# A new written-out order of the words of all engines and of the transfers in a cross-attention kernel

## The chip, the cores and the metric

One Trainium2 chip, one core of it. The metric is the device time of one execution in microseconds (us), the median of the runs shown. The core has five instruction queues that run side by side and wait for one another by semaphores: TensorE (PE, with its weight loads shown apart as PEld), VectorE (DVE), ScalarE (ACT), GpSimd (POOL) and SyncE (SP), which here only issues DMA transfers. Each queue works strictly in its own program order.

## The reference

All arithmetic is float32. `x` is (2, 2048, 640), the context (2, 154, 1024); 77 of its tokens are text, 77 an image prompt. There are 20 heads of 32.

```python
q = _split_heads(hidden_states @ Wq.T, H)
k = _split_heads(text @ Wk.T, H)
v = _split_heads(text @ Wv.T, H)
out_text = _merge_heads(_attend(q, k, v, sm_scale))
k_ip = _split_heads(ip @ Wk_ip.T, H)
v_ip = _split_heads(ip @ Wv_ip.T, H)
out_ip = _merge_heads(_attend(q, k_ip, v_ip, sm_scale))
out = out_text + IP_SCALE * out_ip
out = out @ Wo.T + bo
return out + residual
```

`_attend` is softmax(q kT / sqrt(32)) v. The two softmaxes are taken over the 77 text and the 77 image keys apart.

## The kernel before, in words

Tokens lie in the free dimension, channels in the partitions. The 640 channels are 5 chunks of 128 (4 heads each). A *quarter* q = 0..9 is one batch element and one chunk; a *unit* u = 2q + sub is one half (1024 tokens, two blocks h of 512) of it. The scores of a unit come in three *groups* s = 0, 1, 2 of 3, 3 and 2 tiles of 128 tokens, 4 heads by 154 keys each.

The whole program after a short head (lines 612 to 671) is one string of 1317 *words*, `SCHEDULE` (line 673), split at blanks and handed one by one to `emit` (line 769). A word issues a few instructions on one engine; the order of the words of one engine in the string is the program order of that engine's queue, and the order across engines tells which value of a reused buffer a word reads. `@` and digits after a word name the PSUM banks (0 to 7) that it writes. Nothing else sets the order. The words that matter here:

- TensorE, on full 128x128 weights: `q.u.h` queries of a block (`queries`, L211), `k.c.t` and `v.c.t` keys and values (L146), `g m.p.i` the products of a Strassen-like scheme for later queries (L281, L291), `m m.b.i` those for the output projection of batch element 0 (L579, L589), `o`, `p`, `z` the fifth output chunk (L560), `F` the closing products for batch element 1 (L1006). I call these wide words.
- TensorE, on 32x128 weights: `R s.u` the scores of a group, into four banks (L323). On 32x32 weights: `A.q` probabilities times values (L421).
- ScalarE: `K s.u` copies the scores to SBUF (L335), `E s.u.g` exponentials (L358, L390), `cq`, `ck`, `cv`, `CA`, and some `cg` empty a bank (L232, L826, L828, L444, L300).
- VectorE: `M` maxima (L370, or L373 straight from the bank), `D` sums of the exponentials (L395), `I` their reciprocals (L400), `T` the 32x32 transposes of the probabilities (L412), `cm`, `co`, `Y`, and some `cg` take a bank (L604, L610, L570, L944, L947, L302).
- GpSimd: `S` subtracts the maxima where that is a step of its own (L384), `N` multiplies with the reciprocals (L405).
- *Sums*, plain additions of two SBUF operands: `U` of query weights (L262), `h` of tokens (L275), `W` of output weights (L490), `G` (L520), `V` and `X` (L985, L991) for the closing products. Those that end in `.d` (and with `V`, `X` those with `.d`) are issued on VectorE, all others on GpSimd.
- SyncE, all transfers: `LK`, `LQ`, `LO`, `LW` weights, `LX`, `LH`, `LA`, `SF` tokens in, `SS` results out, `VS` the spreading of the values to the four row groups (8 small DMAs each). The queue issues in order, and a transfer whose place is still in use holds back all behind it.

For one group of scores the chain is R, K, M, (S), E, D, I, N, T, and once all six groups of a quarter have their T, `A`. TensorE keeps busy with wide words between them.

The change and the steps of the prediction touch `SCHEDULE` alone; these functions, as they stand, carry the words that the prediction names: `queries`, `project_kv`, `scores`, `attend`, `pair_product`, `product`, `take_product`, `store_last`, `sum_pair_tokens`, `sum_w`, `subtract`, `normalise`, `maxima`, `load_block`, `load_wq`. The engine of a sum is settled in `emit`:

```python
adder = nc.vector if args and args[-1] == "d" else nc.gpsimd
```

Of the kernel before, what the change touches and what calls it, by code (L numbers as in the profile page):

```python
# [20 lines left out]
def kernel(  # L21
# [643 lines left out]
    for t in range(2):  # L665
# [8 lines left out]
        "q.0.1@2 R0.0@6457 cq.0.1 R1.0@0132 K0.0 K1.0 q.1.0@6 LK.4 M0.0 LK.5 M1.0 S0.0 LQ.3 R2.0@0132 v.0.0@7 K2.0 "  # L674
        "E0.0.0 E0.0.1 E0.0.2 E0.0.3 M2.0 S1.0 q.1.1@2 cv.0.0 D0.0 E1.0.0 S2.0 I0.0 cq.1.1 E1.0.1 v.0.1@7 N0.0 "
        "cq.1.0 E2.0.0 E2.0.1 E2.0.2 E1.0.2 E1.0.3 D1.0 cv.0.1 E2.0.3 R0.1@1326 LK.7 D2.0 LK.6 K0.1 R1.1@4507 I1.0 "
        "I2.0 SQ.0 N2.0 VS.0.0 K1.1 q.3.0@1 M0.1 M1.1 S0.1 R2.1@4507 K2.1 LQ.4 E0.1.0 M2.1 S1.1 VS.0.1 T0.0 cq.3.0 "
        "q.2.1@6 E2.1.0 E0.1.1 k.1.0@1 E1.1.0 N1.0 T2.0 E2.1.1 E0.1.2 E1.1.1 k.1.1@7 ck.1.0 E0.1.3 cq.2.1 E2.1.2 "
        "ck.1.1 E1.1.2 E1.1.3 D1.1 I1.1 v.1.0@6 T1.0 N1.1 E2.1.3 D0.1 cv.1.0 R2.2@5017 LK.10 SF.0.4 R0.2@3246 K2.2 "
        "LK.8 q.3.1@5 LK.9 D2.1 K0.2 I0.1 T1.1 N0.1 I2.1 M0.2 R1.2@3246 q.4.0@7 N2.1 K1.2 T0.1 S0.2 T2.1 M2.2 "  # L680
        "A.0@3246 E0.2.0 M1.2 S2.2 cq.4.0 E0.2.1 E0.2.2 cq.3.1 E0.2.3 D0.2 E2.2.0 S1.2 I0.2 CA.0 R0.3@0175 N0.2 "
        "K0.3 E2.2.1 v.1.1@3 k.2.1@0 E1.2.0 cv.1.1 E2.2.2 LK.13 ck.2.1 E1.2.1 E2.2.3 E1.2.2 D2.2 I2.2 M0.3 "
        "R2.3@6175 SQ.1 SF.0.3 R1.3@2430 S0.3 K2.3 E1.2.3 D1.2 VS.1.1 q.4.1@6 M1.3 E0.3.0 N2.2 M2.3 E1.3.0 k.2.0@5 "
        "T0.2 S2.3 SF.0.1 E1.3.1 v.2.0@7 VS.1.0 T2.2 E2.3.0 E0.3.1 I1.2 ck.2.0 E2.3.1 E0.3.2 E0.3.3 q.5.0@1 D0.3 "
        "N1.2 cv.2.0 E2.3.2 E1.3.2 cq.4.1 E2.3.3 D2.3 E1.3.3 LK.12 I2.3 I0.3 SF.0.2 T1.2 N2.3 LK.11 SF.0.0 cq.5.0 "
# [12 lines left out]
        "N2.7 cq.10.0 LX.10.1 T1.7 LK.18 K0.8 R1.8@7204 S2.8 K1.8 q.9.1@5 M0.8 T2.7 S0.8 LQ.7 M1.8 E0.8.0 S1.8 "
        "cq.9.1 E0.8.1 v.4.1@4 A.3@6720 E2.8.0 E0.8.2 E1.8.0 E2.8.1 E1.8.1 E0.8.3 E1.8.2 E2.8.2 E2.8.3 E1.8.3 D0.8 "
        "I0.8 D2.8 N0.8 cv.4.1 I2.8 CA.3 R0.9@3154 VS.5.0 D1.8 I1.8 G5.0 K0.9 v.4.0@6 T0.8 R2.9@7203 N2.8 cv.4.0 "  # L700
        "q.11.1@5 SQ.4 M2.9 VS.4.0 N1.8 E2.9.0 M0.9 E2.9.1 E2.9.2 T2.8 S0.9 E2.9.3 R1.9@4672 q.10.1@0 M1.9 LX.12.0 "
        "E1.9.0 I2.9 E0.9.0 E0.9.1 E0.9.2 T1.8 N2.9 E1.9.1 q.11.0@3 LX.12.1 VS.4.1 E1.9.2 E0.9.3 D0.9 E1.9.3 I0.9 "
        "T2.9 N0.9 cq.11.1 D1.9 cq.10.1 R0.10@4672 cq.11.0 K0.10 R1.10@1503 I1.9 T0.9 K1.10 g2.0.0@4 g1.0.0@7 "
        "M0.10 U0.0 N1.9 LO R2.10@6215 cg1.0.0 g2.0.1@0 K2.10 h5.0.0 T1.9 E0.10.0 g1.0.1@1 h7.0.0 g5.0.0@5 E0.10.1 "
        "cg2.0.0 U4.0 M2.10 A.4@3624 U1.0 cg1.0.1 E0.10.2 h6.0.0.d h5.0.1.d M1.10 E0.10.3 h7.0.1 U3.0 cg5.0.0 "
        "E2.10.0 h6.0.1.d S1.10 cg2.0.1 E2.10.1 U2.0.d g3.0.0 VS.6.0 CA.4 g5.0.1@0 g6.0.1 h4.0.1 cg5.0.1 D0.10 "
        "E2.10.2 g6.0.0 h4.0.0 R0.11@3624 cg6.0.0 cg6.0.1 I0.10 cg3.0.0 E2.10.3 g7.0.0 M0.11 N0.10 E1.10.0 g7.0.1 "
        "o.0@5 D2.10 E0.11.0 W0 E0.11.1 cg7.0.0 cg7.0.1 T0.10 E0.11.2 E0.11.3 g4.0.0 co.0 SS.0.4 D0.11 cg4.0.0 "
        "E1.10.1 R1.11@3625 LX.13.0 g3.0.1 K1.11 I0.11 g4.0.1 cg3.0.1 I2.10 M1.11 N2.10 cg4.0.1 R2.11@6250 LX.13.1 "
        "R1.12@4731 K2.11 E1.10.2 m2.0@6 S1.11 K1.12 E1.10.3 M2.11 E2.11.0 cm2.0 R0.12@4731 N0.11 T2.10 K0.12 "  # L710
        "R2.12@2506 g1.0.2@4 M1.12 K2.12 m1.0@3 E2.11.1 h5.0.2.d m5.0@6 G6.0 cm1.0 E1.11.0 D1.10 SS.0.0 h7.0.2 "
        "E2.11.2 E1.11.1 E1.11.2 g5.0.2@0 h6.0.2 M2.12 SF.1.0 g1.0.3@5 cg1.0.2 E2.11.3 h5.0.3.d g6.0.2 I1.10 cm5.0 "
        "h7.0.3 cg5.0.2 E1.11.3 g2.0.2@2 D1.11 cg6.0.2 W1 g7.0.2 g2.0.3@1 cg2.0.2 I1.11 h4.0.2 E1.12.0 E1.12.1 "
        "T0.11 m3.0 LQ.9 N1.10 VS.5.1 E2.12.0 cg7.0.2 cg1.0.3 E2.12.1 cg2.0.3 m2.1@2 M0.12 E1.12.2 h6.0.3 T1.10 "
        "N1.11 g4.0.2 E2.12.2 SF.1.4 m6.0 E2.12.3 cm2.1 I2.11 cm3.0 g6.0.3 N2.11 T1.11 g5.0.3@2 cg6.0.3 E0.12.0 "
        "g3.0.2 h4.0.3 T2.11 cg4.0.2 cg5.0.3 E0.12.1 g7.0.3 G7.0 LX.16.0 A.5@7164 cg7.0.3 D2.12 E0.12.2 U0.1.d "
        "E1.12.3 cm6.0 G4.0.d cg3.0.2 I2.12 E0.12.3 N2.12 m7.0 CA.5 D0.12 R0.13@0716 I0.12 cm7.0 N0.12 g3.0.3 "
        "M0.13 E0.13.0 m4.0 LQ.8 E0.13.1 SS.0.1 cg3.0.3 T0.12 h5.1.0 E0.13.2 g4.0.3 E0.13.3 cm4.0 R1.13@0271 U1.1 "
        "cg4.0.3 I1.12 D0.13 SF.1.1 U4.1 K1.13 R2.13@4635 VS.6.1 U3.1 g1.1.0@0 N1.12 g2.1.0@2 cg1.1.0 M1.13 K2.13 "
        "R2.14@7146 g5.1.0@3 K2.14 I0.13 M2.13 h6.1.0 R1.14@5714 cg5.1.0 T2.12 LX.16.1 h7.1.0 E2.13.0 SS.0.3 o.1@6 "  # L720
        "VS.7.0 M2.14 S1.13 E2.13.1 T1.12 K1.14 E1.13.0 G5.1 cg2.1.0 m1.1@4 co.1 U2.1 M1.14 E2.13.2 E1.13.1 N0.13 "
# [12 lines left out]
        "M0.16 cg2.1.2 SS.1.1 g5.1.3@7 T1.16 S0.16 cg6.1.3 R0.17@0514 cg5.1.3 SF.2.1 SS.1.3 g3.1.3 K0.17 D2.16 "
# [320 lines left out]
```

## Time and profile before

| what | value |
| --- | --- |
| median of 3 runs (lowest, highest) | 490.3 us (489.92, 490.32) |
| span of the profiled execution, first to last instruction | 488.8 us |
| median less span | 1.5 us |
| VectorE busy | 427.2 us, 87% |
| GpSimd busy | 374.0 us, 76% |
| ScalarE busy | 342.1 us, 70% |
| TensorE weight loads, beside the matmuls | 312.0 us, 64% |
| DMA moved | 62.86 MB, mean 129 GB/s |
| transfers issued by SyncE | 291 |

The time of the profiled execution is its span and what lies around it; only the median of the runs is known for that, and it is 1.5 us more than the span. Rows of the chain of waits read: start in us, duration in us, what ran (engine, tile, line, matmul records). Each float32 matmul leaves two records. Rows of the groups read: line, engine, operation, out<-in shapes, count, then busy us and mean ns of one, then idle time of the engine before them and what ended it.

### The profile page before, as it was taken

The numbers are of one execution on the slowest core, as the hardware profiler recorded it, in microseconds if no ns is written. First come the engines' busy times: TensorE is split into PE (matmuls) and PEld (weight loads), VectorE is DVE, ScalarE is ACT, GpSimd is POOL, SyncE is SP. The second block draws the span as 40 slices with busy tenths as digits, with TensorE's granted clock in tenths as the row PEclk, the third lists the DMA queues.
The fourth block names the chain that finished last, engine by engine and source line by source line (L and its number), as shares of the span: only waits on it lengthen the run. The fifth ranks groups of instructions, "written<-read, shape, count | busy, mean of one in ns | idle before, by whom it ended". The sixth has DMA issues, their size and how long they took to land.

```text
span 488.8 us, 11001 instructions
## 1 busy us (share of the span) xinstructions
PE 482.8 (99%) x4244; PEld 312.0 (64%) x4244; DVE 427.2 (87%) x450; ACT 342.1 (70%) x1191; POOL 374.0 (76%) x180
## 2 busy tenths in 40 slices
PE   9999999999999999999999999999999999999996
PEld 5556746657757466566887767787677676444443
DVE  0067998998998989999899899999999999899886
ACT  1267948998699868999898899897979995100000
POOL 0068798887858899888797798899899999369910
PEclk9999999999999999999999999999999999999999
DMA  8994332443061761741623256115130169420026
GB/s 281 351 266 108 83 104 76 132 109 94 18 198 29 235 187 27 232 142 32 214 77 115 78 173 207 56 38 160 48 110 27 45 199 332 130 86 1 21 87 235
DMA packets 63828, 62.86 MB, mean 129 GB/s; under 512 B 5408, under 2 KB 47008, under 8 KB 63776
## 3 DMA queue, kind: packets, MB, share of 16 engines
q1 hardware_dynamic: 62768, 60.99, 40.4%
q10 hardware_dynamic: 1008, 1.18, 0.7%
q8 instruction: 33, 0.54, 0.5%
q14 instruction: 19, 0.16, 0.1%
HBM read 48.38 MB, written 10.49 MB: 120 GB/s over the span
## 4 chain that ended last, share of the span: by engine, by line
PE 91%; ACT 4%; DMA 3%; DVE 1%; ACTq 0%; issue 0%; DVEq 0%
PE bank L211 17%; PE bank L1006 12%; PE bank L281 11%; PE bank L323 10%; PE bank L579 10%; PE bank L421 10%; PE bank L146 8%; PE bank L560 7%; PE bank L589 3%; PE bank L291 3%; ACT pb L358 3%; DMA aT<-in_L_xattn_Wk_ip_dram 2%; DMA x<-in_x_dram 1%; DVE mx L370 1%; ACT pb L335 1%; ACT qT L232 0%
## 5 line engine op out<-in xcount | busy, mean ns | idle before, releaser
L405 POOL TENSOR_TENSOR pb<-pb,rden 128x1848 f32<-128x1848 f32 (+1 forms) x60 | 176.2, 2946 | 33.9 <-DVE rden L400 31.2
L384 POOL TENSOR_TENSOR pb<-pb,mx 128x1848 f32<-128x1848 f32 (+1 forms) x32 | 98.9, 3098 | 37.5 <-DVE mx L370 37.3
L370 DVE TENSOR_REDUCE mx<-pb 128x24 f32<-128x1848 f32 (+1 forms) x51 | 92.8, 1830 | 34.6 <-ACT pb L335 34.5
L412 DVE STREAM_TRANSPOSE pb<-pb 128x1920 f32<-128x1920 f32 (+1 forms) x60 | 114.8, 1926 | 2.1 <-POOL pb L405 1.9
L358 ACT ACTIVATE pb<-pb,mx 128x77 f32<-128x77 f32 x368 | 110.8, 374 | 1.3 <-DVE mx L370 1.2
L335 ACT COPY pb<-bank 128x462 f32<-128x462 f32 (+1 forms) x204 | 86.3, 536 | 17.9 <-PE bank L323 17.7
L395 DVE TENSOR_REDUCE den<-pb 128x24 f32<-128x1848 f32 (+1 forms) x47 | 88.7, 1893 | 8.1 <-ACT pb L390 4.7
L390 ACT ACTIVATE pb<-pb 128x1848 f32<-128x1848 f32 (+1 forms) x32 | 52.5, 1645 | 16.5 <-POOL pb L384 16.4
L421 PE MATMUL bank<-pb,v 32*32 32x512 f32 x1600 | 55.2, 597 | 0.1
L358 ACT ACTIVATE pb<-bank,mx 128x77 f32<-128x77 f32 x200 | 51.4, 373 | 3.5 <-DVE mx L373 3.4
L211 PE MATMUL bank<-x,wq 128*128 128x512 f32 x120 | 53.7, 598 | 0.0
L211 PE MATMUL bank<-x,aT 128*128 128x512 f32 x116 | 52.4, 599 | 0.1
L146 PEld LDWEIGHTS bank<-wo_ct,aT 128*128 128x128 f32 x320 | 43.1, 188 | 5.6 <-issue 3.3
L146 PE MATMUL bank<-wo_ct,aT 128*128 128x154 f32 x320 | 45.6, 296 | 0.8 <-DMA aT<-in_L_xattn_Wk_ip_dram 0.5
L421 PEld LDWEIGHTS bank<-pb,v 32*32 32x32 f32 x1600 | 29.2, 103 | 21.5 <-issue 10.6
L281 PE MATMUL bank<-x,wq 128*128 128x256 f32 x160 | 40.9, 386 | 0.0
L211 PEld LDWEIGHTS bank<-x,wq 128*128 128x128 f32 x120 | 22.1, 190 | 25.5 <-issue 24.7
L211 PEld LDWEIGHTS bank<-x,aT 128*128 128x128 f32 x116 | 21.2, 189 | 24.1 <-issue 23.8
L560 PE MATMUL bank<-aT,wo_ct 128*128 128x512 f32 x80 | 36.4, 596 | 0.0
L358 ACT ACTIVATION_READ_ACCUMULATOR pb<-pb,mx 128x1 f32 x168 | 36.1, 215 | 0.0
L323 PEld LDWEIGHTS bank<-kT,qT 32*128 32x128 f32 x768 | 27.4, 184 | 13.0 <-issue 7.3
L281 PEld LDWEIGHTS bank<-x,wq 128*128 128x128 f32 x160 | 29.5, 190 | 6.5 <-issue 2.3
(111 smaller groups left out, 706.2 us busy)
## 6 DMA issues: line engine op xcount, KB each, us to landing
x<-in_x_dram SPq DMA_DIRECT2D x15, 1280.0 KB, 6.6
out_dram<-acc SPq DMA_DIRECT2D x19, 256.0 KB, 3.4
x<-in_x_dram SPq DMA_DIRECT2D x17, 256.0 KB, 5.9
acc<-in_x_dram SPq DMA_DIRECT2D x16, 256.0 KB, 3.4
out_dram<-x SPq DMA_DIRECT2D x15, 256.0 KB, 2.0
aT<-in_L_xattn_Wk_dram SPq DMA_DIRECT2D x5, 512.0 KB, 5.4
aT<-in_L_xattn_Wk_ip_dram SPq DMA_DIRECT2D x5, 512.0 KB, 6.5
aT<-in_L_xattn_Wv_dram SPq DMA_DIRECT2D x5, 512.0 KB, 7.0
```

The lines of the kernel that those rows point to most:

```text
L146: nc.tensor.matmul(keys_in(out), loaded[n][:, k, :], cT[:, k, :, t, :], start=(k == 0), stop=(k == NCC - 1))
L211: nc.tensor.matmul(pq, weight_of(q)[:, k, :], xs[place_of(u, h)][:, k, :], start=(k == 0), stop=(k == NC - 1), skip_group_check=loose,)
L281: nc.tensor.matmul(part, w[m][:, kp], t[m][:, kp], start=(kp == 0 and m in (1, 2, 5)), stop=(kp == 1 and m in (1, 6, 7)), skip_group_check ...
L323: nc.tensor.matmul(ps[g][:, ts(t, 2 * L)], qTs[(u, h)][g * D : (g + 1) * D, ts(st, P)], kT[g * D : (g + 1) * D, c, b].rearrange("p t l -> ...
L335: nc.scalar.copy(keys_of(u, s)[:, :, g], ps[g][:, : n * 2 * L].rearrange("p (n l) -> p n l", n=n))
L358: nc.scalar.activation(row, row if ps is None else rows_in(ps[g], n)[:, t, x], AF.Exp, bias=maxs[(u, s)][:, *one], accum_out=None if den i ...
L370: nc.vector.tensor_reduce(mx, rows_of(u, s), AX.X, ALU.max, negate=negate)
L384: nc.gpsimd.tensor_tensor(rows_of(u, s), rows_of(u, s), maxs[(u, s)].unsqueeze(3).to_broadcast([P, n, 2, L]), ALU.subtract)
L395: nc.vector.tensor_reduce(den_of(u, s), rows_of(u, s), AX.X, ALU.add)
L405: nc.gpsimd.tensor_tensor(rows_of(u, s), rows_of(u, s), rdens[(u, s)].unsqueeze(3).to_broadcast([P, n, 2, L]), ALU.mult)
L412: nc.vector.transpose(p, p)
L421: nc.tensor.matmul(pa[r][g * D : (g + 1) * D, :], v4s[q % 2][rows, g, k, :], zones[rows, :, g, k, :], start=(k == 0), stop=(k == NK - 1),)
```

## The change

Only the string `SCHEDULE` is replaced. Both strings hold 1317 words, and apart from the bank digits they are the same words: the same instructions on the same engines, the same sums on VectorE and on GpSimd, the same places of the sums `X`. 195 words name banks; 34 of them keep theirs. What differs is the order on every engine, the order of the transfers and the banks. The head before the string, the tail after it and `emit` are as before, and both strings end in the same product and addition (`F32.0`, `Y4.0.20`).

Counted in the two strings: the `R` words stand in 46 separate blocks before and in 44 after; the `A` words are 10 either way; in two places of the new string an `A` word follows an `R` word with no wide word between (none before), in four places an `R` word follows an `A` word (five before); the wide words stand in 52 stretches before and in 49 after.

The core of the diff: the opening, the middle, around the tokens of unit 17, and the end.

```diff
-        "q.0.1@2 R0.0@6457 cq.0.1 R1.0@0132 K0.0 K1.0 q.1.0@6 LK.4 M0.0 LK.5 M1.0 S0.0 LQ.3 R2.0@0132 v.0.0@7 K2.0 "
-        "E0.0.0 E0.0.1 E0.0.2 E0.0.3 M2.0 S1.0 q.1.1@2 cv.0.0 D0.0 E1.0.0 S2.0 I0.0 cq.1.1 E1.0.1 v.0.1@7 N0.0 "
...
-        "T2.9 N0.9 cq.11.1 D1.9 cq.10.1 R0.10@4672 cq.11.0 K0.10 R1.10@1503 I1.9 T0.9 K1.10 g2.0.0@4 g1.0.0@7 "
-        "M0.10 U0.0 N1.9 LO R2.10@6215 cg1.0.0 g2.0.1@0 K2.10 h5.0.0 T1.9 E0.10.0 g1.0.1@1 h7.0.0 g5.0.0@5 E0.10.1 "
-        "cg2.0.0 U4.0 M2.10 A.4@3624 U1.0 cg1.0.1 E0.10.2 h6.0.0.d h5.0.1.d M1.10 E0.10.3 h7.0.1 U3.0 cg5.0.0 "
-        "E2.10.0 h6.0.1.d S1.10 cg2.0.1 E2.10.1 U2.0.d g3.0.0 VS.6.0 CA.4 g5.0.1@0 g6.0.1 h4.0.1 cg5.0.1 D0.10 "
...
-        "R1.12@4731 K2.11 E1.10.2 m2.0@6 S1.11 K1.12 E1.10.3 M2.11 E2.11.0 cm2.0 R0.12@4731 N0.11 T2.10 K0.12 "
-        "R2.12@2506 g1.0.2@4 M1.12 K2.12 m1.0@3 E2.11.1 h5.0.2.d m5.0@6 G6.0 cm1.0 E1.11.0 D1.10 SS.0.0 h7.0.2 "
...
-        "cg2.1.1 D0.15 m4.1 E2.15.3 h4.1.1 E1.15.0 I0.15 I2.15 T1.14 N0.15 g4.1.1 E1.15.1 o.2@5 LX.17.1 T0.14 "
-        "E1.15.2 h5.1.2 cg3.1.1 N2.15 cg4.1.1 E1.15.3 cm4.1 co.2 R1.16@0134 h7.1.2 I1.15 SS.2.4 K1.16 R2.16@2756 "
...
-        "Y3.1.01 F32.1 F28.0 Y4.1.20 Y1.1.20 F32.0 Y4.0.20 "
+        "q.0.1@0 cq.0.1 R0.0@1234 R1.0@5670 K0.0 q.1.0@1 K1.0 M0.0 LK.5 LK.4 M1.0 LQ.5 S0.0 LQ.3 v.0.1@2 cq.1.0 S1.0 "
+        "cv.0.1 R2.0@3456 LK.7 R0.1@7012 K2.0 q.1.1@3 E0.0.0 E0.0.1 E0.0.2 E0.0.3 M2.0 S2.0 E1.0.0 E1.0.1 E1.0.2 E1.0.3 "
...
+        "T2.9 E1.9.1 N0.9 cq.10.1 D1.9 cq.11.0 R0.10@5413 R1.10@6270 K0.10 U0.0 I1.9 T0.9 g2.0.0@5 N1.9 K1.10 LO "
+        "g1.0.0@4 M0.10 R2.10@1362 K2.10 g1.0.1@7 h5.0.0 T1.9 g2.0.1@0 E0.10.0 U4.0 U1.0 g5.0.0@1 cg1.0.0 cg1.0.1 "
+        "cg2.0.0 E0.10.2 U2.0.d A.4@3625 h6.0.0.d h5.0.1.d E0.10.1 M2.10 h4.0.0 h7.0.0 cg5.0.0 M1.10 E2.10.3 W0 E0.10.3 "
+        "h6.0.1.d E2.10.2 g6.0.0 D0.10 g6.0.1 cg6.0.0 CA.4 g7.0.0 I0.10 g5.0.1@3 h7.0.1 cg7.0.0 cg2.0.1 cg6.0.1 E2.10.1 "
+        "U3.0 R0.11@6250 cg5.0.1 N0.10 M0.11 g3.0.0 E0.11.0 g3.0.1 E2.10.0 g4.0.0 S1.10 cg3.0.1 cg3.0.0 D2.10 g7.0.1 "
+        "cg4.0.0 LX.13.0 E0.11.1 cg7.0.1 R1.11@6314 I2.10 T0.10 E0.11.3 o.0@2 W1 E0.11.2 h4.0.1 E1.10.0 E1.10.1 E1.10.2 "
+        "E1.10.3 D0.11 N2.10 K1.11 g4.0.1 I0.11 co.0 h5.0.2.d cg4.0.1 R2.11@0563 LX.13.1 M1.11 N0.11 R1.12@1247 SS.0.4 "
+        "K2.11 VS.5.1 m2.0@0 K1.12 M2.11 S1.11 E2.11.0 cm2.0 R0.12@5631 M1.12 R2.12@2470 K0.12 g1.0.2@5 g2.0.2@6 "
...
+        "E0.15.3 h5.1.2 m4.1 I2.15 cg7.1.1 SS.1.1 T0.14 h4.1.1 E1.15.0 N2.15 o.2@0 cg3.1.1 E1.15.3 D0.15 SF.2.1 SF.2.2 "
+        "E1.15.1 I0.15 T2.14 N0.15 E1.15.2 cm4.1 g4.1.1 co.2 R1.16@7352 LX.17.1 cg4.1.1 I1.15 h7.1.2 T0.15 R0.16@6014 "
+        "K1.16 N1.15 g5.1.2@7 M1.16 g1.1.2@3 cg5.1.2 K0.16 g3.1.2 h6.1.2.d cg1.1.2 R2.16@5260 S1.16 T1.15 K2.16 "
+        "g2.1.2@1 g1.1.3@4 T2.15 g6.1.2 cg1.1.3 h5.1.3 M2.16 cg6.1.2 A.7@5260 E1.16.0 E1.16.1 E1.16.2 E1.16.3 G7.2 "
...
+        "F32.1 F16.1 Y4.1.20 Y1.1.20 F9.1 F16.0 Y5.1.21 F9.0 F28.0 Y5.0.21 F32.0 Y4.0.20 "
```

In the opening, `v.0.1` now stands ahead of `v.0.0`, and `LQ.5` comes third of all transfers of the string, with `LQ.4` far behind. In the middle, the queue of VectorE holds `co.0 h5.0.2.d M1.11 M2.11 cm2.0` in this order, while that of GpSimd holds `h4.0.1 N2.10 N0.11 S1.11`; before, `h5.0.2.d` stood behind `M2.12`, well after both.

146 rows, old and new, of the table SCHEDULE are left out of this document.

## The prediction

> **What bounds the kernel now.** I read the page first, then the chain of waits in order of time, then the list of waits, the groups by form, and the timelines of VectorE, GpSimd and ScalarE where the order changes most.
>
> ```profile
> span 488.8 us, 11001 instructions
> PE 482.8 (99%) x4244; PEld 312.0 (64%) x4244; DVE 427.2 (87%) x450; ACT 342.1 (70%) x1191; POOL 374.0 (76%) x180
> ...
> PEclk9999999999999999999999999999999999999999
> ```
>
> TensorE is busy 99% of the span, at full granted clock in every slice. The other engines have 60 to 145 us to spare, so they set the end only where a value of theirs comes late for TensorE. The chain shows in which pieces TensorE works; its columns are start, duration, what ran, number of matmul records.
>
> ```profile
> 17.06 2.38 PE bank L146 x16
> ...
> 33.04 4.29 PE bank L211 x10
> ...
> 39.44 1.78 PE bank L323 x48
> 41.22 4.49 PE bank L211 x10
> ...
> 57.26 1.52 PE bank L323 x40
> ...
> 68.75 5.45 PE bank L421 x150
> 74.21 1.00 PE bank L323 x24
> ...
> 116.50 1.61 PE bank L323 x40
> ...
> 203.52 2.04 PE bank L323 x48
> ...
> 223.27 1.92 PE bank L281 x8
> ...
> 238.88 1.76 PE bank L323 x40
> ...
> 260.71 1.73 PE bank L281 x8
> ...
> 278.78 1.80 PE bank L323 x40
> ...
> 432.56 52.60 PE bank L1006 x124
> ```
>
> From 17.1 us, when the first weights are there, to 485.2 us (432.56 + 52.60) TensorE runs without a hole; the last addition and store take the other 3.6. Neither the part before 17 nor the part after 485 changes: the head is the same, and both orders end in `F32.0 Y4.0.20`. So the time is the length of 468 us of matmuls, and an order can change it in two ways only: by turns between kinds of matmuls, and by waits.
>
> The turns can be read off the pieces. Ten records of L211 take 4.29 between key and value words (33.04) and 4.49 between score words (41.22): a stretch of wide words pays 0.20 for its two ends. L281 agrees: eight records take 1.73 among their like, 1.92 between score blocks. Scores: 24 records take 1.00 alone, 48 take 1.78; a further word costs 0.78, so the block itself pays 0.22. The 5.45 of `A` is the same in every piece.
>
> The waits are what is longer than its like: 203.52 (2.04 for 1.78), 116.50, 238.88 and 278.78 (1.61, 1.76 and 1.80 for 1.52), together 0.26 + 0.09 + 0.24 + 0.28 = 0.9 us. The list of waits names what came last in these (columns: total us, times, longest):
>
> ```profile
> PEld bank L323 <- ACT pb L358: 1.8, 3, 0.8
> PEld bank L323 <- ACT qT L232: 1.8, 2, 1.0
> ...
> PEld bank L421 <- DVE pb L412: 1.1, 2, 0.8
> ```
>
> These are waits of weight loads and partly hidden behind the matmul before. So little is left: even if the new order had no wait at all, waits would give about 1 us.
>
> **The change part by part.** *Removed and added work: none.* Both strings hold the same 1317 words, so every busy time stands, and so does every duration but where two sums meet.
>
> *Turns.* The wide words stand in 52 stretches before and 49 after, the score words in 46 blocks before and 44 after, the `A` words are ten either way. Saved are 3 x 0.20 + 2 x 0.22 = 1.04 us, all on the path, as TensorE is the path. One boundary has no row: twice in the new order an `A` follows scores directly. The nearest is the score block behind an `A` (74.21), which at 1.00 pays the full 0.22 of a block between wide words. I take the same for the other direction. From below, the end toward an `A` could be free (half of 0.22 each, 0.2 in all to the gain); from above, it costs what a wide stretch's end does besides (0.10 each, 0.2 in all to the loss). So the turns give 0.8 to 1.3. The Trainium skill (TensorEngine Tiling (Array Packing), Key Properties) says that changing the tiling mode drains TensorE; by that rule these two boundaries are mode changes like the others, and the sum would be the middle value. No run here shows them yet.
>
> *Waits that stay or move.* `R1.10` still follows `cq.10.1 cq.11.0` at once (the wait at 203.52), and `R2.12` still needs the bank that `cm2.0` empties (238.88). The waits at 116.50 and 278.78 lose their cause, as other words stand between. New tight places of the same kind come in: in three more places a short third group follows a first one and the next wide word then takes the bank just copied (`q.4.0`, `v.3.0`, `q.11.1`). Each is bounded by what such a place costs now, 0 to 0.28; I take 0.12, nearest to the 0.09 at 116.50, since a bank that is copied first is nearly free by then. So 0.37 are saved and 0.36 come back: nothing.
>
> *Transfers.* `v.0.1` moves ahead of `v.0.0` and needs the last weights of the head.
>
> ```profile
> aT<-in_L_xattn_Wv_ip_dram SPq DMA_DIRECT2D x1, 512.0 KB, 7.9
> ...
> L136 SPq DMA_DIRECT2D aT<-in_L_xattn_Wv_ip_dram x2: 368/487/606, 20.4 to 39.5; - x2
> ...
> x<-in_x_dram SPq DMA_DIRECT2D x15, 1280.0 KB, 6.6
> ```
>
> They were issued at 20.4 and landed at 28.3. In the new order TensorE reaches `v.0.1` at 17.06 + 2.2 (keys) + 4.4 (`q.0.1`) + 1.8 (two score words) + 4.4 (`q.1.0`) = 29.8: covered by 1.5 us. `LX.17.1` can be issued once `g4.1.1` has read its place, and `g1.1.3` needs it. Between these TensorE did `o.2` and some 5.1 us more, 9.5 in all; now `o.2` stands ahead of `g4.1.1`, and what is left is two scores in one block (1.8), `g5.1.2`, `g1.1.2`, `g3.1.2` (16 records of 0.216, two ends: 3.7), a third group (0.7) and `g2.1.2` (1.4): 7.6 against a median landing of 6.6. I cost it at nothing; if that cover of 1.0 fails, its price is what the landing exceeds 7.6. `SF.2.1` and `SF.2.2` stand ahead of it on SyncE's queue now and wait for results to be stored, but those are due 11 us of TensorE earlier. `LQ.5` third of all delays the transfers behind it by a 320 KB load, about 1 us; its neighbours `LK.7` and `LK.6` are needed 20 us later.
>
> *Sums of VectorE and GpSimd.* What such a meeting costs now:
>
> ```profile
> 216.80 3.62 POOL L384 TENSOR_TENSOR pb<-pb,mx 128x1848 f32<-128x1848 f32 x1
> ...
> 217.53 3.17 DVE L262 TENSOR_TENSOR wq<-wq,wq 128x256 f32<-128x256 f32 x1
> ...
> 132.89 1.60 ACT L358 ACTIVATE pb<-pb,mx 128x77 f32<-128x77 f32 x6 [0.51 <-DVE mx L370]
> ```
>
> ```profile
> L405 POOL TENSOR_TENSOR pb<-pb,rden 128x1848 f32<-128x1848 f32 x40 | 131.5, 3290 | 24.0 <-DVE rden L400 22.0 <-ACT qT L300 1.8
> ...
> L370 DVE TENSOR_REDUCE mx<-pb 128x24 f32<-128x1848 f32 x33 | 67.7, 2060 | 30.7 <-ACT pb L335 30.7
> ...
> L405 POOL TENSOR_TENSOR pb<-pb,rden 128x1232 f32<-128x1232 f32 x20 | 45.2, 2258 | 9.9 <-DVE rden L400 9.2 <-ACT pb L335 0.7
> ...
> L370 DVE TENSOR_REDUCE mx<-pb 128x16 f32<-128x1232 f32 x18 | 25.4, 1408 | 3.9 <-ACT pb L335 3.8
> L335 ACT COPY pb<-bank 128x308 f32<-128x308 f32 x72 | 24.8, 437 | 8.5 <-PE bank L323 8.5
> ...
> L275 POOL TENSOR_TENSOR x<-x 128x512 f32<-128x512 f32 x15 | 19.3, 1291 | 2.9 <-DVE v_sb L275 2.8
> ...
> L604 DVE SCALAR_TENSOR_TENSOR acc<-bank,bo_sb,acc 128x256 f32<-128x256 f32 x32 | 13.3, 458 | 1.9 <-PE bank L589 1.9
> ...
> L570 DVE SCALAR_TENSOR_TENSOR res<-bank,bo_sb,res 128x512 f32<-128x512 f32 x4 | 3.0, 738 | 1.1 <-PE bank L560 1.1
> ...
> L275 DVE TENSOR_TENSOR x<-x,v_sb 128x512 f32<-128x512 f32 x4 | 2.9, 721 | 0.0
> ...
> L262 DVE TENSOR_TENSOR wq<-wq 128x256 f32<-128x256 f32 x1 | 0.4, 415 | 0.0
> ```
>
> `U2.0.d` is a sum of 0.42 us; begun at 217.53 inside a subtraction of GpSimd that ended at 220.42, it ended at 220.70: it stood 2.75 us. VectorE had room, so it cost TensorE nothing. Where the new order takes such meetings off, TensorE therefore gains nothing by that alone. The question is whether it has one with no room behind it. I find one pair, and it is the rival below.
>
> *The sum.* By its own span the new execution takes 488.8 - 1.0 = 487.8; the median of the runs lies 1.5 above the span, and the transfers and the code around it are the same, so 490.3 - 1.0 = 489.3.
>
> **The rivals.** *A sum of VectorE loses its turn (slower).* In the new order VectorE's queue holds `co.0 h5.0.2.d M1.11 M2.11 cm2.0`, GpSimd's `h4.0.1 N2.10 N0.11`. Counted from the end of `R2.10`: TensorE reaches the end of `o.0` after 16, 18 and 22 records of 0.216 in three stretches (12.7 with their ends), `A.4` 5.45, two single scores 2.0 and `o.0` 4.4, 24.5 us; with `co.0` (0.74, and some 0.1 to begin) `h5.0.2.d` asks at 25.4. GpSimd: the four copies of `K2.10`, six exponentials, `cg1.0.0`, `cg2.0.0`, `U2.0.d`, `h6.0.0.d`, `h5.0.1.d` in a row, 1.3 + 1.5 + 0.3 + 0.3 + 0.35 + 2 x 0.62 = 5.0, each by its row less the 0.1 by which neighbours of a queue overlap (six exponentials take 1.60); then without a gap four `h`, three `W0`, two `W1` and `U3.0` (about 11.7 at 1.29 and less), `N0.10`, `S1.10` (3.29 each) and `N2.10` (2.26), less 13 overlaps of 0.04, plus one turn of VectorE (0.6): 20.6. `N2.10` ends at 25.6. The sum asks 0.2 us before `N0.11` would begin and gets the turn between them. If it asks later, it stands for 3.29, and with it all behind it: 0.8 + 3.3 + 0.7 + 2.1 + 1.4 + 0.9 = 9.2 from `o.0` to the end of `cm2.0`. `R2.12` needs that bank and is due after `g4.0.1` (1.4), a block of two scores (1.5), `m2.0` (12 records and ends, 2.8) and `R0.12` (0.9), 6.6: TensorE stands 2.6. `K0.12`, behind exponentials that wait for `M2.11`, adds up to 0.9, so I take 3.0: 492.3 us. The point from which it decides is the 0.2 us. For it speaks that 0.2 is small beside two counts of 25; against it, that every part left out on GpSimd's side (a wait of its own, a second turn) makes the margin larger. The Trainium skill (SBUF — State Buffer, Who interferes with whom) says the same: of a VectorE instruction with two SBUF inputs and a GpSimd one that reads SBUF, the first to start keeps the port to its end. The trace agrees, 2.75 us above. By this rule the time is 489.3 or 492.3 and nothing between.
>
> *The waits take it back (no change).* Several places become tight by 0.1 to 0.3 each, as shown by the score pieces now; with four more than I count, 1.0 is given back: 490.3. For it speaks that the whole order is new; against it, that the old one, of the same density, has 0.9 in all.
>
> *The waits go too (faster still).* Without the 0.9 as well: 488.4.
>
> *The change does not do what it says.* Then sums still meet; that is the first rival, or costs nothing, as `U2.0.d` did.
>
> **How the numbers follow.** Forecast 0.62, the lost turn 0.18, waits take it back 0.12, waits go too 0.08. The forecast's own range is 488.6 to 490.2: the turns' 0.8 to 1.3, and the new places between 0 and 0.28 each, with the kept waits gone or doubled. Within 0.2% (0.98 us, about what a measurement of this kernel can tell from no change) means 489.3 to 491.3, and the forecast lies on that edge: of its 0.62 I put 0.34 below and 0.28 inside. Faster is 0.34 + 0.08 = 0.42. Inside are 0.28 and 0.08 of the third case, 0.36; slower is 0.18 and the rest of that case, 0.22. The range must reach toward the lost turn, since without it more than 2 in 10 are left out: 488.3 to 492.3.
>
> **What would show it.** Right: the chain has fewer pieces of L323, wide pieces of 4.49 become 4.29 or longer merged ones, the last record ends near 484.1, the span is near 487.8, VectorE's sum of tokens `h5.0.2.d` (L275) near 232 us is short. The rival: a VectorE row of L275 of about 4 us beside an L405 on GpSimd there, and 2 to 3 us idle of TensorE at `R2.12`, near 239 us, put down to `acc` L604. Wrong as well: waits of TensorE for L193 or L162 transfers, or pieces of L421 longer than 5.45.

## The result, and the profile after

The changed kernel takes 494.7 us in the median of six runs (492.80 to 494.96), the one before 490.1 (489.90 to 491.53): a ratio of 1.0076, 95% interval 1.0057 to 1.0095. It is slower by 0.8%, outside the predicted range. The changed kernel's runs lie on two levels, 492.8 (two of six, mean granted clock 1.000) and 494.7 to 495.0 (four of six, 0.996 to 0.997); the profiled one, 492.82, is of the first, so its page shows the loss without the part that the clock adds.

The page, in its lines of span, busy time and the slices of TensorE:

```profile
span 491.0 us, 11000 instructions
...
PE 482.5 (98%) x4244; PEld 314.8 (64%) x4244; DVE 428.2 (87%) x450; ACT 342.1 (70%) x1191; POOL 374.5 (76%) x180
...
PE   9999999999999999999899999999999999999996
```

The busy times stand; the span is 2.2 longer. TensorE has one slice of 8 instead of 9, the one around 239 us. The timeline of VectorE shows what comes just before:

```profile
233.58 0.30 DVE L400 RECIPROCAL rden<-den 128x24 f32<-128x24 f32 x1
233.80 0.65 DVE L570 SCALAR_TENSOR_TENSOR res<-bank,bo_sb,res 128x512 f32<-128x512 f32 x1
234.37 3.52 DVE L275 TENSOR_TENSOR v_sb<-x 128x512 f32<-128x512 f32 x1
237.81 3.41 DVE L370 TENSOR_REDUCE mx<-pb 128x24 f32<-128x1848 f32 x2
241.14 0.86 DVE L604 SCALAR_TENSOR_TENSOR acc<-bank,bo_sb,acc 128x256 f32<-128x256 f32 x2
```

The columns are start, duration, engine, line and operation. The third row is `h5.0.2.d`, 3.52 us long where such a sum takes 0.7. The timeline of GpSimd, with the idle time before an instruction in brackets:

```profile
231.13 2.24 POOL L405 TENSOR_TENSOR pb<-pb,rden 128x1232 f32<-128x1232 f32 x1
234.05 3.29 POOL L405 TENSOR_TENSOR pb<-pb,rden 128x1848 f32<-128x1848 f32 x1 [0.68 <-ACT pb L335]
```

These are `N2.10` and `N0.11`. The second began 0.32 us ahead of the sum, and the sum ended 0.55 after it. What matters is when `N0.11` began: not when `N2.10` ended (233.37), but 0.17 after `I0.11` ended on VectorE (233.88), whose reciprocals it multiplies with. The releaser in brackets is not the one: ScalarE's copy is only what the profile saw last. In VectorE's own queue `I0.11` stands two words ahead of the sum.

What it cost shows in the timeline of TensorE:

```profile
239.01 1.32 PE L323 MATMUL bank<-kT,qT 32*128 32x154 f32 x30
242.05 0.79 PE L323 MATMUL bank<-kT,qT 32*128 32x154 f32 x10 [1.73 <-DVE acc L604]
243.21 1.99 PE L281 MATMUL bank<-x,wq 128*128 128x256 f32 x8 [0.37 <-ACT pb L335]
```

From the start of this block of two score words, `R0.12 R2.12`, to the next wide word it is 4.20 us; a block of two takes 1.52. I call the difference the stand at `R2.12`: 2.68 here, 0.24 before. It has two waits in a row: first for `cm2.0`, which ended at 242.00, then for ScalarE's copy `K0.12`, which stood behind exponentials that waited for the late maxima.

The chain of waits names a second place, which I had not found:

```profile
212.37 1.82 DVE v_sb L275
214.19 3.33 DVE mx L370 x2
217.52 0.96 DVE x L275
...
218.62 2.99 PE bank L281 x12
```

Here TensorE's `g6.0.1` waits for `h6.0.1.d`, which is late because `h5.0.1.d`, at 212.37, took 1.82 instead of 0.7. GpSimd at that moment (timeline):

```profile
212.36 2.98 POOL L275 TENSOR_TENSOR x<-x 128x512 f32<-128x512 f32 x2 [1.58 <-DVE x L275]
```

The end of `h6.0.0.d` let `h4.0.0` go on GpSimd and `h5.0.1.d` on VectorE; GpSimd began 0.01 us earlier, and VectorE stood 1.1 (1.82 for 0.69). The length from the start of `g6.0.0` (216.71) to that of `g3.0.0` (222.97) is 6.26 us; without these waits it is 5.16 (shown below), so this place cost 1.1.

So at full clock: 490.1 - 1.0 for the turns + 2.4 + 1.1 = 492.6, against 492.8 measured. What makes it 494.7 in most runs is a third thing, the clock.

### The profile page after: what moved, and what is told of

Same layout as the page of the kernel before. It is cut to its first block, busy times and chain, and to the rows that moved or that the text cites. A ratio compares the mean times of both kernels' runs of the same rounds, so it can differ in the third digit from the quotient of the medians.

```text
span 491.0 us, 11000 instructions
## 1 busy us (share of the span) xinstructions
PE 482.5 (98%) x4244; PEld 314.8 (64%) x4244; DVE 428.2 (87%) x450; ACT 342.1 (70%) x1191; POOL 374.5 (76%) x180
## 4 chain that ended last, share of the span: by engine, by line
PE 51%; DVE 3%; ACT 1%; issue 0%; DVEq 0%
PE bank L1002 12%; PE bank L579 10%; PE bank L281 9%; PE bank L560 6%; PE bank L421 6%; PE bank L323 4%; PE bank L589 3%; PE bank L291 2%; DVE mx L370 1%; ACT pb L358 1%; DVE v_sb L275 1%; DVE den L395 0%; DVE x L275 0%; DVE res L570 0%; ACT pb L335 0%; DVE acc L943 0%
## 5 line engine op out<-in xcount | busy, mean ns | idle before, releaser
L358 ACT ACTIVATE pb<-bank,mx 128x77 f32<-128x77 f32 x200 | 52.4, 382 | 3.4 <-DVE mx L373 3.2
L421 PEld LDWEIGHTS bank<-pb,v 32*32 32x32 f32 x1600 | 31.6, 103 | 18.8 <-issue 8.1
L281 PE MATMUL bank<-x,wq 128*128 128x256 f32 x160 | 41.3, 387 | 1.1 <-DVE x L275 0.8
L211 PEld LDWEIGHTS bank<-x,wq 128*128 128x128 f32 x120 | 22.2, 190 | 25.9 <-issue 25.4
L281 PEld LDWEIGHTS bank<-x,wq 128*128 128x128 f32 x160 | 29.3, 190 | 9.8 <-issue 3.5
```

What stands on the lines that cost most here:

```text
L211: nc.tensor.matmul(pq, weight_of(q)[:, k, :], xs[place_of(u, h)][:, k, :], start=(k == 0), stop=(k == NC - 1), skip_group_check=loose,)
L281: nc.tensor.matmul(part, w[m][:, kp], t[m][:, kp], start=(kp == 0 and m in (1, 2, 5)), stop=(kp == 1 and m in (1, 6, 7)), skip_group_check ...
L358: nc.scalar.activation(row, row if ps is None else rows_in(ps[g], n)[:, t, x], AF.Exp, bias=maxs[(u, s)][:, *one], accum_out=None if den i ...
L421: nc.tensor.matmul(pa[r][g * D : (g + 1) * D, :], v4s[q % 2][rows, g, k, :], zones[rows, :, g, k, :], start=(k == 0), stop=(k == NK - 1),)
```

## Experiments

Each kernel was timed beside the kernel before on the same chip (490.0 to 490.7 there). The diffs show the moved words as they stand in the string; all others keep their order.

**1. The sum ahead of what releases its rival.** After, with one word moved:

```diff
- D0.11 N2.10 K1.11 g4.0.1 I0.11 co.0 h5.0.2.d cg4.0.1 R2.11@0563
+ D0.11 N2.10 K1.11 g4.0.1 co.0 h5.0.2.d I0.11 cg4.0.1 R2.11@0563
```

> After, with one word moved: the reciprocals I0.11 stand behind h5.0.2.d instead of ahead of co.0, so that the product N0.11 on GpSimd, which I0.11 releases, can begin only after the sum has been taken. Theory (lost turn): h5.0.2.d falls from 3.5 to 0.7 us, TensorE's excess at R2.12 from 2.68 to under 0.3, the profiled time from 492.82 to 490.2 to 490.5; the 0.94 at g6.0.1 stays. Rival (the place is tight in the new order whoever has the turn: R2.12 and g1.0.2 need banks that cm2.0 and K0.12 empty behind long queues): the excess there stays over 1.5 and the time over 491.8. On the second level of the times (granted clock 0.996 to 0.997 in four of six runs of after, 2 us longer): if it comes with the long stall of TensorE, no run of this kernel shows it; if it comes with something else in the new order, most runs do, near 492.3.

Measured: 490.36 us (11 runs, 489.63 to 490.68; ratio to before 1.0003, 0.9995 to 1.0012); the profiled run 490.20. VectorE's and then TensorE's timeline:

```profile
234.00 0.68 DVE L275 TENSOR_TENSOR v_sb<-x 128x512 f32<-128x512 f32 x1
```

```profile
238.83 1.82 PE L323 MATMUL bank<-kT,qT 32*128 32x154 f32 x40
240.58 1.78 PE L281 MATMUL bank<-x,wq 128*128 128x256 f32 x7
```

The sum takes 0.68; the stand is 240.58 - 238.83 - 1.52 = 0.23. The lost turn is the cause of the 2.4, and no run has a mean clock under 0.999. This is no faster than before: the 1.0 of the turns and the 1.1 of the other place cancel, which experiment 5 tests.

**2. The sum next behind what releases its rival.** After, with `co.0` moved, so that the sum follows `I0.11` at once:

```diff
- D0.11 N2.10 K1.11 g4.0.1 I0.11 co.0 h5.0.2.d cg4.0.1 R2.11@0563
+ D0.11 N2.10 K1.11 g4.0.1 I0.11 h5.0.2.d co.0 cg4.0.1 R2.11@0563
```

> After, with one word moved: co.0 behind h5.0.2.d, so that VectorE has I0.11 h5.0.2.d co.0. I0.11 still releases N0.11 on GpSimd, but the sum is now the next on its own queue. In the trace N0.11 starts 0.47 us after the start of I0.11, the next instruction of VectorE 0.21 after it. Theory (the first to start has the turn to its end): the sum wins by 0.26, takes 0.7, N0.11 starts 0.4 later, the excess at R2.12 is 0.25, and the time is that of the kernel with I0.11 moved, 490.3 +- 0.2, plus at most 0.2 where R1.12 waits for co.0. Rival (GpSimd has the turn whenever both want it within some tenths): the sum stands 3 us, 492.8 or with the half clock 494.7.

Measured: 490.19 us (11 runs; 1.0003, 0.9994 to 1.0012). VectorE, then GpSimd:

```profile
233.65 0.30 DVE L400 RECIPROCAL rden<-den 128x24 f32<-128x24 f32 x1
233.87 0.63 DVE L275 TENSOR_TENSOR v_sb<-x 128x512 f32<-128x512 f32 x1
```

```profile
234.13 3.52 POOL L405 TENSOR_TENSOR pb<-pb,rden 128x1848 f32<-128x1848 f32 x1 [0.63 <-ACT pb L335]
```

Now `N0.11` is the one that stands: it begins 0.26 after the sum and its row is 3.52 long instead of 3.28. The wait for a turn lies inside the row's duration, not in its idle time. So a lead of 0.26 us decides for VectorE here, as one of 0.32 did for GpSimd in after.

**3. The same loss made in the kernel before.** Before, with one word moved ahead of three others of VectorE, `cm2.0`, `T2.10` and `M1.12` (it stood directly behind `M1.12`, not behind `M2.12`, as the section on the change and the expectation have it):

```diff
- K2.11 E1.10.2 m2.0@6 S1.11 K1.12 E1.10.3 M2.11 E2.11.0 cm2.0 ... m1.0@3 E2.11.1 h5.0.2.d m5.0@6
+ K2.11 E1.10.2 m2.0@6 S1.11 K1.12 E1.10.3 M2.11 E2.11.0 h5.0.2.d cm2.0 ... m1.0@3 E2.11.1 m5.0@6
```

> Before, with one word moved: h5.0.2.d ahead of cm2.0 instead of behind M2.12. In the trace of before M2.11 ends at 238.17 and S1.11 holds GpSimd until 239.54; so by the theory of the lost turn the sum stands from 238.2 to 239.5, is done at 240.1, cm2.0 ends 1.2 us later than now, and the excess at R2.12 grows from 0.24 to 1.4: 491.3 to 491.5 against 490.1. Rival (a sum behind a GpSimd instruction costs TensorE nothing in itself, the new order around it does): 490.1 to 490.3.

Measured: 491.30 us (8 runs; 1.0024, 1.0014 to 1.0034). VectorE, GpSimd, TensorE (this profile starts 1.0 us earlier than that of before):

```profile
237.05 2.00 DVE L275 TENSOR_TENSOR v_sb<-x 128x512 f32<-128x512 f32 x1
```

```profile
235.22 3.29 POOL L384 TENSOR_TENSOR pb<-pb,mx 128x1848 f32<-128x1848 f32 x1
238.46 3.74 POOL L405 TENSOR_TENSOR pb<-pb,rden 128x1848 f32<-128x1848 f32 x1
```

```profile
237.78 1.32 PE L323 MATMUL bank<-kT,qT 32*128 32x154 f32 x30
239.90 0.79 PE L323 MATMUL bank<-kT,qT 32*128 32x154 f32 x10 [0.80 <-DVE acc L604]
240.61 1.13 PE L281 MATMUL bank<-x,wq 128*128 128x256 f32 x4
```

As expected, the sum stood until GpSimd's subtraction ended near 238.5; the stand is 240.61 - 237.78 - 1.52 = 1.31, for 1.4 expected. When GpSimd's instruction ended, both engines wanted the turn; VectorE, which had waited, got it, and `N0.11` paid 0.45 (3.74 for 3.29). Order alone, in a kernel with none of the rest of the change, makes the loss.

**4. The other place, by its last wait.** After, with `h6.0.1.d` earlier on VectorE:

```diff
- h7.0.0 cg5.0.0 M1.10 E2.10.3 W0 E0.10.3 h6.0.1.d E2.10.2 g6.0.0
+ h7.0.0 cg5.0.0 h6.0.1.d M1.10 E2.10.3 W0 E0.10.3 E2.10.2 g6.0.0
```

> After, with one word moved: h6.0.1.d ahead of the maxima M1.10 instead of behind them. Theory: g6.0.1 stands 0.94 because h5.0.1.d loses 1.2 us to h4.0.0 on GpSimd and h6.0.1.d stands behind it and behind 3.4 us of maxima; asked before the second maxima it is ready when g6.0.1 is due, so that excess goes to under 0.15 and the profiled time from 492.82 to 491.9 +- 0.2, with 2.7 still lost at R2.12. Rival (the sum meets W0 there as well and loses as much): 492.8. On the clock: the stall of 2.7 stays, so if the second level comes with it, some of these runs show 0.996 to 0.997 and 2 us more.

Measured: 494.12 us (six runs, 492.25 to 495.04; 1.0075, 1.0058 to 1.0092), no gain over after. The expectation failed. The same word, moved together with that of experiment 1:

> After, with both words moved (I0.11 behind h5.0.2.d, h6.0.1.d ahead of M1.10). Theory (the two sums are all that the new order lost): 492.82 - 2.4 to 2.7 - 0.9 = 489.2 to 489.5 at full clock, about 0.8 below before, which is the gain by fewer turns (1.0) less what small waits keep. Rival (the losses are made up of many tight places that follow one another): more than 491. If the second level of the clock belongs to the stalls, it is gone here.

Measured: 490.50 us (11 runs; 1.0009, 1.0000 to 1.0017), no gain over experiment 1 either. TensorE's timeline of this kernel shows why:

```profile
216.63 1.99 PE L281 MATMUL bank<-x,wq 128*128 128x256 f32 x8
219.53 1.10 PE L281 MATMUL bank<-x,wq 128*128 128x256 f32 x4 [0.91 <-ACT qT L300]
```

`g6.0.1` now follows `g6.0.0` without a gap (8 records in a piece), and the next product, `g7.0.0`, waits as long for ScalarE's copy `cg6.0.0`, behind 14 exponentials that wait for the maxima `M2.10`. The moved sum itself met `W0` on GpSimd and took 1.66 instead of 0.7, as the rival of the first expectation had it, but TensorE no longer waited for it. I mended that too, by letting the copies go ahead of some exponentials:

```diff
- E0.10.3 E2.10.2 g6.0.0 D0.10 g6.0.1 cg6.0.0 CA.4 g7.0.0
+ E0.10.3 g6.0.0 D0.10 g6.0.1 cg6.0.0 CA.4 E2.10.2 g7.0.0
```

> The kernel with both words moved, and one more: the exponentials E2.10.2 stand behind the copies CA.4 instead of ahead of g6.0.0, so that ScalarE reaches cg6.0.0 1 us earlier (its 14 exponentials in a row before that copy become 10). Theory: g7.0.0 stood 1.07 for this copy, which was hidden behind the wait for the sum as long as that was as late; now the excess around g6.0.1 and g7.0.0 is under 0.3 in all, the profiled time 490.37 - 0.9 = 489.4 or less, and the median 0.7 to 1.0 below that of before: the turns' gain of 1.0 stands alone. Rival (a third wait lies behind these two, at g5.0.1 for CA.4, or the exponentials come late for D2.10 and what follows): 490.0 to 490.6.

Measured: 490.33 us (11 runs; 1.0005, 0.9996 to 1.0014). The third wait is there, one word on (TensorE):

```profile
216.80 3.03 PE L281 MATMUL bank<-x,wq 128*128 128x256 f32 x12
...
222.17 1.05 PE L323 MATMUL bank<-kT,qT 32*128 32x154 f32 x18 [0.58 <-DVE qT L302]
```

All three products run as one piece of 12 records, and `R0.11` waits for a copy of VectorE instead. Three mends of three waits gained nothing: what they may share is that VectorE's queue, and by its maxima ScalarE's, runs some 1.1 us late from 212.4 on. The next experiment tests this.

**5. The other place, by its first cause.** The kernel of experiment 1, with GpSimd's `h7.0.1`, which may begin only when `h5.0.1.d` is done, ahead of `h4.0.0`:

```diff
- h5.0.1.d E0.10.1 M2.10 h4.0.0 h7.0.0 ... g5.0.1@3 h7.0.1 cg7.0.0
+ h5.0.1.d E0.10.1 M2.10 h7.0.1 h4.0.0 h7.0.0 ... g5.0.1@3 cg7.0.0
```

> The kernel with I0.11 moved, and on GpSimd the sum h7.0.1 ahead of h4.0.0 (it stood behind the three sums of W0). h7.0.1 overwrites what h5.0.1.d reads, so GpSimd begins its row of sums only when h5.0.1.d is done, instead of in the same instant (212.36 and 212.37 us in after). Theory: all three waits that took one another's place here (g6.0.1 for the sum, g7.0.0 for ScalarE's copy, R0.11 for VectorE's copy) come from the 1.2 us that h5.0.1.d stands, which puts back VectorE's queue and, by the maxima, ScalarE's; with it at 0.7 instead of 1.8 us all three are gone, the excess from g6.0.0 to g3.0.0 falls from 1.1 to 0.3 or less, and the median is 0.8 below that of the kernel with I0.11 moved: 489.4 to 489.6, 0.5 to 0.8 below that of before. That would be the turns' gain of 1.0 less the small waits. Rival (TensorE comes to this place too early for any order of the sums: the stretch before it lost words to later ones): 490.2 to 490.5 again, with a fourth wait.

Measured: 489.22 us (8 runs, 488.74 to 489.77; ratio to before 0.9966, 0.9954 to 0.9979): faster than both kernels. VectorE, and then pieces of the chain:

```profile
212.76 0.69 DVE L275 TENSOR_TENSOR v_sb<-x 128x512 f32<-128x512 f32 x1
```

```profile
17.23 2.38 PE bank L146 x16
...
54.91 1.03 PE bank L323 x24
...
56.52 4.56 PE bank L211 x10
...
67.48 1.00 PE bank L323 x24
68.48 5.45 PE bank L421 x154
...
104.52 0.74 PE bank L323 x16
105.25 5.53 PE bank L421 x149
...
203.25 1.78 PE bank L323 x48
...
278.34 1.96 PE bank L323 x47
...
431.94 52.38 PE bank L1002 x124
```

The sum takes 0.69, and from the start of `g6.0.0` to that of `g3.0.0` it is 222.32 - 217.16 = 5.16 us in TensorE's timeline, where after has 6.26. TensorE's whole path, from the first key words to the end of the products, is 431.94 + 52.38 - 17.23 = 467.09; before it was 432.56 + 52.60 - 17.06 = 468.10. The difference is 1.01; the second profile of experiment 6 has 467.09 as well (430.65 + 52.38 - 15.94). By the runs the gain is less sharply known: the kernel before took 490.71 beside this one, 1.5 more, and the interval of the ratio allows 1.0 to 2.3.

**6. One loss brought the other.** After, with the move of experiment 5 alone: `I0.11 co.0 h5.0.2.d` stand as in after.

> After, with h7.0.1 ahead of h4.0.0 on GpSimd and nothing else: I0.11 co.0 h5.0.2.d stand on VectorE as in after. Theory (one loss brought the other about): with the first loss gone, VectorE's sums D0.11 begin 0.7 us earlier against GpSimd, which does its row of sums 0.7 later, as in the run with both moved (D0.11 230.80 to 232.88, N2.10 to 234.11). So I0.11 is done near 233.2, while GpSimd still has N2.10; h5.0.2.d asks near 233.8, is the one that waits when N2.10 ends, has the turn before N0.11, stands 0.3 us instead of 2.9, and R2.12 stands 0.25: 489.2 to 489.6 in the median, as with both moved. Rival (GpSimd's next instruction, released before, goes on without giving the turn up; or the place at R2.12 is lost by the order of VectorE's words alone): the sum stands 3 us, 491.6 to 491.9 at full clock and 493.7 with the half clock.

Measured: 489.52 us (12 runs; 0.9982, 0.9970 to 0.9993). Eleven runs lie between 488.42 and 490.27; the profiled one took 492.96, and there the sum did lose. VectorE, and GpSimd:

```profile
234.29 3.74 DVE L275 TENSOR_TENSOR v_sb<-x 128x512 f32<-128x512 f32 x1
```

```profile
209.55 1.28 POOL L275 TENSOR_TENSOR v_sb<-x 128x512 f32<-128x512 f32 x1 [0.66 <-DMA v<-v_sb]
...
231.98 5.50 POOL L405 TENSOR_TENSOR pb<-pb,rden 128x1232 f32<-128x1232 f32 x2
```

The second row of GpSimd holds `N2.10` and `N0.11` without a gap; `N2.10` (2.26) ended near 234.2, and the sum asked at 234.29. In this run a spreading of values had come 0.66 late at 209.55, and TensorE had lost 0.6 us there. The same kernel, run again:

> The same kernel as the run before (h7.0.1 ahead of h4.0.0 alone), for a second profile. In the first profile N2.10 ended near 234.24 and the sum asked at 234.29, behind a load that had put TensorE back by 0.6 us at 209 us; it stood 3.1 us and that run took 492.96, while the other eleven lay between 488.42 and 490.27. Theory (whoever asks first after N2.10's end has the turn, and the margin is some tenths): in a profile without that late load the sum asks before N2.10 ends, stands under 0.5, R2.12 stands 0.25, and the time is 489.5 +- 0.8. Rival (the sum loses here in every run, and the eleven shorter times have another cause): the sum stands 3 us again in a run of 490 or less.

Measured: 489.44 us (5 runs; 0.9973, 0.9956 to 0.9989), the profiled run 488.48. VectorE, and GpSimd:

```profile
232.47 0.95 DVE L275 TENSOR_TENSOR v_sb<-x 128x512 f32<-128x512 f32 x1
```

```profile
230.62 5.95 POOL L405 TENSOR_TENSOR pb<-pb,rden 128x1232 f32<-128x1232 f32 x2
```

Here the sum asked 0.4 before `N2.10` ended, stood 0.3 and went between the two products, whose pair is 0.45 longer. One word on GpSimd, 20 us earlier, removes both losses in 16 of these 17 runs by their times; in the other one a load was 0.66 late and the second came back. Only two of the 17 were profiled, one of each kind, so that the late load is the reason is argued from one profile and not tested. The kernel of experiment 5, where the order of VectorE's words settles it, has no such run among eight.

**7. The clock.** To see whether the two levels of after come from the long stand itself, I made the stand in the kernel of experiment 1 with no sum losing a turn, by letting other VectorE words, `M1.12` and `T2.10`, go ahead of `cm2.0`:

```diff
- M2.11 S1.11 E2.11.0 cm2.0 R0.12@5631 M1.12 R2.12@2470 ...
+ M2.11 S1.11 E2.11.0 R0.12@5631 M1.12 T2.10 cm2.0 R2.12@2470 ...
```

> The kernel with I0.11 moved, and on VectorE M1.12 and T2.10 (2.0 and 1.4 us) ahead of cm2.0: TensorE's stand at R2.12 is made again, as long as in after, but by a queue, with no sum that loses a turn. The copy ends 2.6 us later than at 239.8, so the excess at R2.12 grows from 0.23 to 2.8, and the time at full clock from 490.3 to 492.9. If the second level of the times (granted clock half for some 3.3 us behind the stand) follows from the length of TensorE's stand, some half of these runs or more are 1.6 to 2.2 us longer again, near 494.8, at a mean clock of 0.996 to 0.997; if it follows from the two engines contending, or from something else of the new order, all lie at 492.9 and a mean clock of 0.999 to 1.

Measured: 494.66 us (four runs, 494.37 to 495.57, clocks 0.996 and 0.997; ratio 1.0099, 1.0084 to 1.0115). With `D1.10` in the place of `T2.10`:

> The same with M1.12 and D1.10 (2.0 and 2.1 us) ahead of cm2.0: excess at R2.12 3.4, time at full clock 493.5. If the half clock follows from the length of the stand, a larger share of the runs than in after (four of six) shows it, near 495.4 and a mean clock of 0.996; if not, none.

Measured: 496.57 us (four runs, 495.84 to 497.16, clock 0.996 once and 0.993 three times; 1.0132, 1.0118 to 1.0145). The stands came out 0.4 longer than I had worked out, 3.23 and 3.82 (243.07 - 238.32 - 1.52 for the first), and every run shows the low clock. What it looks like is in the profile of experiment 4's first kernel, which fell on the lower level (494.17). First TensorE, then stretches of one and three us: from and to, length, busy time (and number of instructions) of PE, PEld, DVE, ACT and POOL, then the granted clock, the DMA share and GB/s:

```profile
238.66 1.32 PE L323 MATMUL bank<-kT,qT 32*128 32x154 f32 x30
241.71 0.79 PE L323 MATMUL bank<-kT,qT 32*128 32x154 f32 x10 [1.72 <-DVE acc L604]
242.86 2.88 PE L281 MATMUL bank<-x,wq 128*128 128x256 f32 x8 [0.37 <-ACT pb L335]
```

```profile
243.00:244.00 1.00, 1.00 (x5) 0.89 (x6) 1.00 (x2) 1.00 (x3) 0.00 (x0) 0.91 0.09 21
244.00:245.00 1.00, 1.00 (x4) 0.82 (x3) 1.00 (x1) 1.00 (x5) 0.88 (x1) 0.50 0.10 22
245.00:246.00 1.00, 1.00 (x4) 0.73 (x4) 0.86 (x2) 1.00 (x6) 1.00 (x2) 0.50 0.15 39
246.00:247.00 1.00, 1.00 (x4) 0.82 (x3) 1.00 (x1) 1.00 (x8) 1.00 (x2) 0.50 0.13 35
247.00:250.00 3.00, 3.00 (x15) 2.60 (x14) 1.94 (x5) 3.00 (x10) 2.07 (x2) 0.96 0.11 30
```

The stand is the same 2.68 as in after's profile, with the same two idle times. But 1 us after TensorE has gone on, its clock is half: eight records of L281 take 2.88 for the 1.99 of after. The half clock lasts (0.09 + 3 x 0.50 + 3 x 0.04) / 0.5 = 3.4 us, which leaves 1.7 us of work undone, most of the 1.9 between the two levels of after. By the length of the stand, each taken from one profile: 1.31 (experiment 3) shows a mean clock under 0.998 in none of 8 runs, 2.68 (after, and experiment 4's first kernel) in 8 of 12, 3.23 in 4 of 4, 3.82 in 4 of 4. The odd run of experiment 6 stood 2.91 (243.36 - 238.93 - 1.52) and kept the full clock, so near 2.7 to 2.9 both outcomes occur. The half clock comes with a long stand, and no sum that loses its turn there is needed for it. Why the longest stand cost three runs another 0.003 of mean clock no trace shows; a second stretch at half clock would fit.

The Trainium skill (TensorE: Matmul & The Clock Gate, What's actually happening) says that the array's clock is halved after an idle window of about 3.4 us, and that the windows run freely, whatever the kernel does. The half clock, its length of 3.4 us and the chance from run to run agree with that. The Trainium skill (TensorE: Matmul & The Clock Gate, HAM oscillation — how this bites in real kernels) asks for no idle gaps above about 3.4 us; here two gaps of 1.7 and 0.4 us, 2.1 in all, were enough in most runs, and the measurement decides.

## Why the prediction was wrong

*Bound by TensorE, time set by turns and waits*: right. Every difference of these kernels is found on TensorE's path.

*Turns, 1.04 us*: right. Once neither of the two sums stands long, the path is 1.01 shorter than before, and the kernel of experiment 5 takes 489.22, where 489.3 was forecast; that the two times agree to 0.1 is closer than the runs can tell. The boundary that had no row, an `A` directly behind scores, pays the full price, the middle value that I took: the single score word ahead of `A.0` takes 1.00 and `A.0` its 5.45, that ahead of `A.1` 0.74 and `A.1` 5.53. A sign that I had named against myself did show: five of the ten pieces of `A` take 5.48 to 5.66 in the chain of experiment 5, where before's chain has one, of 5.51.

*Small waits, 0.37 saved and 0.36 back*: near in their sum, as 1.04 and 1.01 leave 0.03 for them, but place by place not as I said, so that is in part luck. In experiment 5 the wait at 203.52, which was to stay, is gone (1.78 at 203.25); the one at 278.78, which was to go, leaves 0.18 (1.96 for 1.78 at 278.34); and the new place ahead of `q.4.0` costs 0.16 where I took 0.12 (56.52 - 54.91 - 1.52, and 4.56 for 4.49).

*Transfers, nothing*: right for the order as such: in after's list of waits no matmul behind the head waits for a transfer. In the one odd run of experiment 6 a late spreading came ahead of the lost turn.

*"I find one pair, and it is the rival below"*: this is the step that failed. In the sum of the forecast such meetings stand at nothing; they cost 1.1 + 2.4 us, more than the turns gained. There were two pairs. I looked for a sum that asks while GpSimd has something long, and passed over `h5.0.1.d` and `h4.0.0`, which are let go by the same instruction, `h6.0.0.d`, and begin within 0.01 us of each other. That pair cost 1.1 by itself. It also bears on the other: my count put the end of `N2.10` 25.6 us after `R2.10`, and the run has it at 25.7 (207.68 to 233.37); it put the sum's request at 25.4, and the run has it 1.3 later (234.37). Of this the first loss is 1.1: without it, in the second profile of experiment 6, the request comes 25.6 after `R2.10` (206.84 to 232.47), and the sum wins by 0.4, where the count had 0.2. The request also follows something that I left out: `co.0` began behind `I0.11` (done at 233.88), and not behind `o.0` (done at 233.47).

*What `N0.11` waits for*: also wrong. I let it follow `N2.10` and never asked when `I0.11` is done. Once `N2.10` is out of the way, `I0.11` releases it, from two words ahead of the sum in VectorE's own queue, and in after it began 0.32 ahead of the sum.

*The price of the rival, 3.0, and its time, 492.3*: the price was near (the stand is 2.68, 2.44 more than before, with `K0.12` behind `cm2.0` as I had it). That 492.3 comes within 0.5 of the runs at full clock, 492.8, is in part luck: 0.6 too much for the stand makes up for half of the 1.1 of the first pair, which I did not have. In most runs 1.9 for the half clock come on top, so the time was neither 489.3 nor 492.3. No rival had the clock; nothing in the profile of before, without a stand over 0.3 us behind its head, could show it. The chance of 0.18 was too low for a margin of 0.2 us between two counts of 25 us each, of which one had a hole.

## What to carry to other kernels

For every plain sum on VectorE, ask which instruction releases the nearest instruction of GpSimd. Where the same instruction released both, the sum lost in all eight profiles with that order; where the releaser stood two words ahead of the sum in VectorE's queue, the sum lost in after (it won in experiment 6 where it asked while GpSimd was still busy), and directly behind the releaser it won, by 0.26 us. An order of words that settles who is first is worth more than a counted margin of some tenths. When one mended wait makes place for the next of the same size, look for the queue that is late as a whole and follow it back to where it became so. And count a long stand of TensorE at more than its length: here 2.7 us cost 4.4 or more in 8 of 12 runs.

## What the runs showed of the hardware that was not expected

Beside the half clock: who has the turn between VectorE's and GpSimd's sums followed a lead of 0.01 us (212.36 and 212.37) in one place, in all eight profiles with that order, and of 0.26 in another, and the engine that already waits goes next (experiments 3 and 6). Whether 0.01 us decides, or GpSimd has the turn when both ask at once, no run separates. The Trainium skill (SBUF — State Buffer, Who interferes with whom) says that whoever issues first holds the port for the whole instruction; these rows agree, as finely as they can be read.
